# First attention of a two-layer network: norms, projections and tiles written as one hand order, output projected by tiles of 128 tokens

## The chip, the cores and the metric

The kernel runs on one core of a Trainium2 chip. The metric is the device time of one execution in microseconds (us); a single run's time and a median of several runs are both used below and always named. The core's engines run side by side, each with an instruction queue of its own that is worked off in order: TensorE (PE, matrix products; its weight loads are listed apart as PEld), VectorE (DVE), ScalarE (ACT), GpSimd (POOL), and SyncE (SP), which here only issues DMAs. PE writes to PSUM, which has eight banks of 128 partitions by 512 float32.

## What is computed

`x` has 2 sequences of 1024 tokens with 128 features, all float32. Eight residual stages follow one another: `x = x + stage(layernorm(x))`. The change touches the first only, a local attention with 16 heads of 8 features and windows of 64 tokens:

```python
def _L0_attn_a_ref(x, Wq, bq, Wk, bk, Wv, bv, Wo, bo):
    W, H = 64, 16; dh = D // H; C = L // W; scale = 1 / sqrt(dh)
    q, k, v = x @ Wq.T + bq, x @ Wk.T + bk, x @ Wv.T + bv
    # each window of 64 queries sees its own 64 keys and the 64 before them
    idx = arange(C)[:, None] * W + arange(2 * W)[None, :]
    kc, vc = (padded by W in front)[:, idx]
    scores = einsum('bcqhd,bckhd->bchqk', qc, kc) * scale   # keys before token 0 masked
    out = einsum('bchqk,bckhd->bcqhd', softmax(scores), vc)
    return out @ Wo.T + bo
```

The other seven stages (a mixture of experts, a causal attention, the experts again, a second small attention, six transformer layers, a linear attention, six layers again) stay as they are.

## The kernel before

`network` (L1712) reads `x` into four tiles `xt` of 128 features by 512 tokens (a "block"), loads the early weights, and calls the stages in turn; `attn_a0` is the first, `ffn0` follows. Most stages already write out by hand in which order each engine's instructions go (`tc.manual_schedule`); outside such a section the framework's scheduler sets the order.

`attn_a0` has two parts. The first is under the scheduler and runs over the four blocks: a layer norm (PE turns the block over to PSUM, DVE takes mean and variance, ACT a square root and DVE its reciprocal at L172 and L173, DVE subtracts and scales at L181, PE turns it back, ACT copies it to `a0xn`); the projection to queries and keys (L239), brought to SBUF with their biases by ACT (L241) and DVE (L243) as `a0both`; a DMA of `a0both` to DRAM (`a0rows`, L245) and eight DMAs back (`a0qk`, L248) that put every head's 8 features at the start of a 32 partition group; the values (L255), brought to SBUF with their bias by DVE (L259).

The second part is `Chunks`, by hand. It runs over 16 tiles of 128 tokens, 8 to a sequence, as a pipeline of calls:

- `scores`: 64 small matmuls (L874) into four banks (PSUM tag `sc`, four buffers, so one tile's scores at a time; the projections use the same tag).
- `softmax`, in two halves: per bank a maximum (L886) and a subtraction (L887) on DVE, with a mask added first (L884) in the first tile of a sequence; then an exponential of half a tile on ACT (L889).
- `sums`: DVE sums the tile (L894) and takes reciprocals (L895), POOL multiplies the two halves (L897).
- `transposes`: four times four PE transposes into a bank of tag `tp` (two buffers) and a copy by ACT to `a0pT` (L201, L907).
- `outputs`: 64 small matmuls into a bank of their own (two in turn, L918), and a copy by ACT to `a0oT` (L924).
- `project`, every fourth tile only: eight 512 column matmuls (L931) into a `tp` bank, and one DVE instruction (L933) that adds bias and result to a block's `xt`.

The probabilities `a0pr` have three buffers: tile m's can be written once tile m-3's have been transposed. In iteration n of the loop the calls are softmax(n), project(n-3), transposes(n-2), sums(n-1), scores(n+1), outputs(n-2).

Of the kernel before, what the change touches and what calls it, by code (L numbers as in the profile page):

```python
# [10 lines left out]
F32 = mybir.dt.float32  # L11
BF16 = mybir.dt.bfloat16
AF = mybir.ActivationFunctionType
ALU = mybir.AluOpType
# [3 lines left out]
P = 128  # L18
# [66 lines left out]
class Net:  # L85
# [118 lines left out]

    def attn_a0(self, key):
        nc, tc = self.nc, self.tc
        scale = 1.0 / math.sqrt(DH)  # L210
        with ExitStack() as ctx:
            wp = ctx.enter_context(tc.tile_pool(name="a0w", bufs=1))
            sb = ctx.enter_context(tc.tile_pool(name="a0s", bufs=2))
            ps = ctx.enter_context(tc.tile_pool(name="a0ps", bufs=2, space=PSUM))
            wp2 = ctx.enter_context(tc.tile_pool(name="a0av", bufs=1, space=PSUM))
            dr = ctx.enter_context(tc.tile_pool(name="a0d", bufs=4, space=bass.MemoryType.DRAM))
            w, bv, mask = self.w["a0"], self.w["a0_bv"], self.w["a0_mask"]
            wqk = w[:, 0:256].rearrange("p (s e) -> p s e", s=2)
            wv = w[:, 256:384]
            wo = w[:, 384:896].rearrange("p (g e) -> p g e", g=4)  # L220
            bqk, bo = w[:, 896:898], w[:, 898:899]

            def blk(b, k):
                return slice(WIN + 512 * k, WIN + 512 * (k + 1))

            xn, qk, v = [], [], []
            for b in range(B):
                xn.append(wp.tile([P, WIN + N], F32, tag=f"xn{b}", name=f"a0xn{b}"))
                qk.append(wp.tile([P, 4, 2, WIN + N], F32, tag=f"qk{b}", name=f"a0qk{b}"))
                v.append(wp.tile([P, N // WIN, D], F32, tag=f"v{b}", name=f"a0v{b}"))  # L230
                nc.gpsimd.memset(xn[b][:, 0:WIN], 0.0)
                nc.gpsimd.memset(qk[b][:, :, 1, 0:WIN], 0.0)
            for b in range(B):
                for k in range(2):
                    self.norm(self.xt[2 * b + k], xn[b][:, blk(b, k)], ps, f"{key}_{b}_{k}")
                    both = sb.tile([P, 2, 512], F32, tag="both", name=f"a0both{b}{k}")
                    for s in range(2):
# [26 lines left out]
            for av in avs:  # L264
                nc.vector.memset(av, 0.0)
# [558 lines left out]
    def ffn1(self, key):  # L824
        with ExitStack() as ctx:
            Layers(ctx, self, key).run()


class Chunks:


# [1044 lines left out]
```

## Time and profile before

| what | us |
|---|---|
| median of 3 runs | 4017.5 (4013.72 to 4019.96) |
| the profiled execution: time | 4017.42 |
| the profiled execution: span | 4015.3 |
| first statistics on DVE (L162) start | 12.73 |
| first score of tile 0 on PE (L874) starts | 42.70 |
| first mask of tile 0 on DVE (L884) starts | 45.36 |
| last reciprocal of tile 15 (L895) starts, takes | 189.62, 0.25 |
| last addition to `xt` (L933) starts, takes | 203.15, 0.75 |
| first transpose of the next stage (L1002) starts | 203.96 |

A page of the profile lists busy time by engine, the chain of work that ended last (each step goes back to what released it), and groups of instructions by line. A line of the timeline has the start, the busy time, engine, line, operation, `out<-in`, and in brackets how long the engine sat idle before it and what ended that. A line of the stretches has start and end, length, then busy time and number of instructions of PE, PEld, DVE, ACT and POOL, the clock granted to TensorE (1.00 is full), the share of time that the 16 DMA engines were busy, and GB/s.

### The profile page before, as it was taken

What the parts mean: (1) busy time and instruction counts of PE and PEld (TensorE: products, weight loads), DVE (VectorE), ACT (ScalarE), POOL (GpSimd) and SP (SyncE); (2) the same over time, 40 slices, a digit from 0 to 9 for tenths busy, and PEclk for the clock granted to TensorE, in tenths of its full rate; (3) what the DMA queues carried; (4) which work ended last, traced back from release to release, by engine and by line L of the source; (5) the groups of instructions that cost most, each with busy time, mean ns of one, the idle gap of its engine ahead of it and who ended that gap; (6) DMA issues with size and microseconds to landing.
All of it is one profiled execution on the core that took longest, in us unless ns stands there. A gap on an engine that the chain in (4) does not pass through costs nothing.

```text
span 4015.3 us, 156131 instructions
## 1 busy us (share of the span) xinstructions
PE 3837.7 (96%) x67292; PEld 2518.4 (63%) x67292; DVE 3132.5 (78%) x6004; ACT 2418.4 (60%) x4588; POOL 2492.4 (62%) x1614
## 2 busy tenths in 40 slices
PE   6798979999999999999999879999999999999998
PEld 4545435666666666666666436666666666666665
DVE  6876777888887888878787577787878787878786
ACT  3534437766666666666666447666666666666665
POOL 1432338776766676767765267766766767667662
PEclk8899989999999999999999779999999999999999
DMA  3020322232232332322222022332322323322222
GB/s 87 2 68 17 73 73 60 70 87 74 71 91 69 76 86 74 85 70 74 69 70 68 12 86 69 76 85 75 86 71 74 92 67 77 83 75 69 65 68 55
DMA packets 217398, 281.11 MB, mean 70 GB/s; under 512 B 52494, under 2 KB 108683, under 8 KB 216587
## 3 DMA queue, kind: packets, MB, share of 16 engines
q1 hardware_dynamic: 216714, 271.12, 26.7%
q8 instruction: 536, 8.78, 0.9%
q14 instruction: 148, 1.20, 0.1%
HBM read 69.46 MB, written 3.28 MB: 18 GB/s over the span
## 4 chain that ended last, share of the span: by engine, by line
PE 86%; DVE 7%; DMA 2%; ACT 2%; issue 1%; POOL 1%; SPq 0%; DVEq 0%; POOLq 0%; ACTq 0%
PE pj_l L1358 17%; PE y_l L1589 9%; PE pv_l L1460 9%; PE tqk_l L201 9%; PE av_l L1557 8%; PE sc_l L1507 7%; PE tpr_l L201 4%; PE to_l L201 4%; PE fy_l L1699 3%; PE fg_l L1663 3%; PE fa_l L1684 3%; PE sc_l L1498 2%; DMA f0share_e<-f0d_e 1%; DVE a0pr L887 1%; DVE a0mx L886 1%
## 5 line engine op out<-in xcount | busy, mean ns | idle before, releaser
L1387 DVE TENSOR_TENSOR t_l<-pj_l,rot_l 128x512 f32<-128x512 f32 x1536 | 967.7, 684 | 368.5 <-ACT sq_l L1367 356.9
L1404 POOL TENSOR_TENSOR raw_l<-t_l,t_l 128x1024 f32<-128x1024 f32 x384 | 908.4, 2366 | 527.2 <-DVE on_l L1565 356.3
L1358 PE MATMUL pj_l<-wqkv_l,x_l 128*128 128x512 f32 x1536 | 784.9, 614 | 6.7 <-DVE t_l L1387 4.0
L1419 POOL TENSOR_TENSOR raw_l<-raw_l,rn_l 128x1024 f32<-128x1024 f32 x384 | 723.1, 1901 | 94.5 <-ACT rn_l L1414 87.0
L1393 POOL TENSOR_TENSOR sq_l<-sq_l 128x512 f32<-128x512 f32 x384 | 490.8, 1278 | 310.7 <-ACT sq_l L1367 307.5
L1367 ACT ACTIVATE sq_l<-pj_l 128x512 f32<-128x512 f32 x768 | 461.5, 603 | 367.8 <-PE pj_l L1358 360.5
L201 PE MATMUL tqk_l<-ident_sb,raw_l 128*128 128x128 f32 x3072 | 452.5, 278 | 15.3 <-POOL raw_l L1419 13.6
L1437 ACT COPY qT_l<-tqk_l 128x512 f32<-128x512 f32 x384 | 224.8, 585 | 387.0 <-PE tqk_l L201 386.8
L201 PEld LDWEIGHTS tqk_l<-ident_sb,raw_l 128*128 128x128 f32 x3072 | 356.1, 142 | 160.2 <-issue 122.1
L1460 PE MATMUL pv_l<-wqkv_l,x_l 128*128 128x512 f32 x768 | 415.8, 623 | 5.9 <-DVE ln_xn_fl L1643 5.4
L1589 PE MATMUL y_l<-outT_l,wo_l 128*128 128x128 f32 x3072 | 393.7, 281 | 0.0
L1507 PEld LDWEIGHTS sc_l<-kT_l,qT_l 64*32 64x32 f32 x24576 | 295.4, 105 | 155.2 <-issue 144.8
L1589 PEld LDWEIGHTS y_l<-outT_l,wo_l 128*128 128x128 f32 x3072 | 357.5, 191 | 18.2 <-issue 1.0
L1358 PEld LDWEIGHTS pj_l<-wqkv_l,x_l 128*128 128x128 f32 x1536 | 256.1, 192 | 172.0 <-issue 111.6
L1557 PE MATMUL av_l<-vw_l,pT_l 64*32 64x64 f32 x24576 | 359.9, 224 | 2.1 <-issue 1.9
L1469 ACT COPY v_l<-pv_l 128x512 f32<-128x512 f32 x384 | 225.1, 586 | 224.6 <-PE pv_l L1460 204.1
L1565 DVE TENSOR_TENSOR on_l<-av_l,inv_l 128x512 f32<-128x512 f32 x384 | 247.5, 686 | 119.5 <-PE av_l L1557 119.2
L1557 PEld LDWEIGHTS av_l<-vw_l,pT_l 64*32 64x32 f32 x24576 | 294.2, 105 | 70.0 <-issue 63.2
L1507 PE MATMUL sc_l<-kT_l,qT_l 64*32 64x64 f32 x24576 | 329.7, 223 | 0.0
L201 PEld LDWEIGHTS tpr_l<-ident_sb,pr_l 128*128 128x128 f32 x1536 | 189.1, 141 | 152.1 <-issue 116.4
L1517 DVE TENSOR_TENSOR pr_l<-sc_l,mx_l 128x512 f32<-128x512 f32 x384 | 265.5, 692 | 13.2
L1516 DVE TENSOR_REDUCE mx_l<-sc_l 128x8 f32<-128x512 f32 x384 | 261.4, 681 | 3.3 <-PE sc_l L1507 3.3
(319 smaller groups left out, 6111.9 us busy)
## 6 DMA issues: line engine op xcount, KB each, us to landing
vw_l<-v_l SPq DMA_DIRECT2D x3024, 64.0 KB
wqkv_l<-in_Wqkv SPq DMA_DIRECT2D x36, 512.0 KB
f0share_e<-f0d_e SPq DMA_DIRECT2D x64, 256.0 KB
rot_l<-in_rotary SPq DMA_DIRECT2D x24, 512.0 KB
wo_l<-in_Wo SPq DMA_DIRECT2D x12, 512.0 KB
w_l<-in_W SPq DMA_DIRECT2D x12, 341.0 KB
a0rows<-a0both SPq DMA_DIRECT2D x4, 512.0 KB
a0qk<-a0rows SPq DMA_DIRECT2D x32, 64.0 KB
```

The costliest lines, as they stand in the source:

```text
L201: self.nc.tensor.transpose(tp[:, c, :], src(c), self.ident)
L1358: self.nc.tensor.matmul(pj.rearrange("p h d -> p (h d)"), self.x[b][0][:, ts(a, P)], self.w[i]["qkv"][:, ds(INNER * s + 512 * u, 512)], st ...
L1367: self.nc.scalar.activation(st["sq", s][:, u], st["pj", s, u], AF.Square)
L1387: self.nc.vector.tensor_tensor(to, st["pj", s, u], tabs[:, k, None, ts(w, LD // 2)].to_broadcast(half), ALU.mult)
L1393: self.nc.gpsimd.tensor_tensor(sq[:, 0], sq[:, 0], sq[:, 1], ALU.add)
L1404: self.nc.gpsimd.tensor_tensor(r.rearrange("p h u d -> p u h d"), st["t1", s], st["t2", s], ALU.add)
L1419: self.nc.gpsimd.tensor_tensor(r, r, st["rn"][:, ts(s, LH), None].to_broadcast([P, LH, LD]), ALU.mult)
L1460: self.nc.tensor.matmul(pj, self.x[b][0][:, ts(a, P)], self.w[i]["qkv"][:, ds(2 * INNER + 512 * r, 512)], start=True, stop=True,)
L1507: nc.tensor.matmul(sc[j][ts(c, 32), hp, :], st["q"][rows, hp, ts(c, 32)], st["k"][rows, hp, ds(32 * c, 64)], start=False, stop=(hp == 7),)
L1517: nc.vector.tensor_tensor(p, st["sc"][j], mx[:, :, None].to_broadcast([P, 8, 64]), ALU.subtract)
L1557: nc.tensor.matmul(av[r][ts(c, 32), q, j, :], st["pT", j][rows, q, ts(c, 32)], st["vw"][rows, c, ts(2 * q + j, LD)], start=True, stop=True,)
L1589: self.nc.tensor.matmul(y[:, 0:P], self.w[i]["o"][:, c, :], st["o"][:, c, :], start=(c == 0), stop=(c == 7))
```

## The change

`Chunks` takes over the first part too. Every piece of work of one engine becomes a method with a short name, and a string `A0_ORDER` lists them all; inside the hand-ordered section each engine works off its own words in that order. Words end in the block (0 to 3) or tile (0 to 15), and where there are several pieces in a letter: `sf`, `tp`, `cp` have four (a to d), `ex`, `ml`, `pv`, `ev` two.

- PE: `Tin`, `Tx` (the norm's transposes), `pk`, `pq` (keys and queries), `pv` (values), `S` (scores), `tp`, `av` (outputs), `y` (output projection).
- DVE: `sta`, `dev` (norm), `ek`, `ev` (keys and values out of PSUM), `sf` (mask, maximum, subtraction of one bank), `sm` (sum, reciprocal), `ya` (addition to `xt`).
- ACT: `fx` (norm to SBUF), `eq`, `ex` (exponential), `cp` (copy to `a0pT`), `oc` (copy of the outputs). POOL: `rs` (inverse root), `ml` (product). SP: `dw` (to DRAM), `dl` (eight DMAs back).

What differs beside the order: the norm's inverse root is taken by POOL with a power instead of by ACT and DVE; the maxima of each bank get a small tile of their own; the outputs are copied to a tile of 128 tokens (two buffers) and projected tile by tile, 16 times eight 128 column matmuls, each with a DVE addition of 128 columns; the bank for it is one of the two `tp` banks as before. The two output banks are set to zero at the start. Numbers of buffers are otherwise the same.

```diff
     def attn_a0(self, key):
-        nc, tc = self.nc, self.tc
-        scale = 1.0 / math.sqrt(DH)
         with ExitStack() as ctx:
-            wp = ctx.enter_context(tc.tile_pool(name="a0w", bufs=1))
...
-            avs = [wp2.tile([P, 4, P], F32, tag=f"av{i}", name=f"a0av{i}") for i in range(2)]
-            for av in avs:
-                nc.vector.memset(av, 0.0)
-            with tc.manual_schedule(engines=ORDERED):
-                Chunks(self, [x[:, :, 0, WIN:] for x in qk], [x[:, :, 1, :] for x in qk], v, wo, bo, avs, mask, scale, sb, ps).run()
+            chunks = Chunks(ctx, self)
+            with self.tc.manual_schedule(engines=ORDERED):
+                chunks.run()
...
+A0_ORDER = """
+    Tin0 Tin1 sta0 rs0 dev0 Tx0 fx0 pk0 sta1 ek0 pq0 rs1 dev1 pv0b Tin2 Tx1 eq0 dw0 fx1 pv0a pk1
+    ev0b sta2 pq1 rs2 ev0a pv1a ek1 dl0 dev2 ev1a pv1b eq1 Tin3 Tx2 ev1b sta3 S0 sf0d sf0c ex0b
+    sf0b fx2 sf0a S1 dw1 rs3 dev3 sf1a ex0a Tx3 sf1d fx3 sf1b pq3 sf1c eq3 S2 sm0 ml0b ex1a ex1b
+    sf2a sf2b pk2 tp0d ml0a ek2 pq2 sf2c cp0d dl1 tp0b cp0b eq2 pv2b tp0a tp0c cp0a ex2a sf2d ev2b
+    sm1 S3 sf3b cp0c ex2b sf3a sf3c ml1a sf3d tp1b av0 sm2 cp1b ml1b tp1d ex3a ml2a cp1d ex3b tp1c
+    S4 cp1c sf4c tp1a tp2b sf4a cp1a sf4b cp2b pv3a ev3a ml2b tp2a tp2d sf4d oc0 sm3 cp2a dw2 tp2c
+    S5 sf5a sf5b ml3b sf5c ex4b av1 ml3a pv2a cp2d tp3a cp2c ex4a cp3a sf5d dl2 y0 ev2a tp3b S6 sm4
+    ex5b cp3b ml4b oc1 av2 ya0 sf6d sf6b ex5a tp3c tp3d cp3c cp3d tp4c tp4d cp4c cp4d y1 sf6c sf6a
+    ml4a tp4b ex6a S7 oc2 sm5 ya1 av3 ml5b sf7d tp4a cp4b cp4a y2 sf7c tp5c sf7a pk3 av4 ex6b sf7b
+    ml5a ex7a ek3 ya2 S8 sm6 cp5c ex7b ml6b tp5b tp5a cp5b oc3 dw3 cp5a sf8c tp5d cp5d ml6a sf8b
+    tp6b oc4 cp6b y3 sf8d sf8a tp6c cp6c ex8a ya3 av5 S9 tp6d tp6a sm7 ml7a cp6a cp6d ex8b tp7a
+    sf9b sf9c ml7b cp7a y4 sf9d tp7c ya4 cp7c dl3 sf9a ex9b tp7d sm8 oc5 S10 av6 tp7b ex9a cp7d
+    ml8a tp8a ml8b cp7b oc6 tp8b sf10c av7 cp8a sf10b sf10d tp8d cp8b sf10a sm9 S11 cp8d tp8c sf11d
+    sf11b y5 sf11c ml9b cp8c ex10b ml9a av8 ya5 ex10a tp9c tp9b sf11a cp9c cp9b sm10 tp9d S12 ml10b
+    cp9d ml10a oc7 tp9a cp9a y6 av9 sf12d ex11a oc8 ya6 ex11b tp10c tp10d cp10c sf12a sf12b cp10d
+    tp10a sf12c sm11 tp10b ml11b cp10b S13 cp10a y7 sf13d y8 ex12b ya7 sf13b ex12a ml11a ya8 av10
+    tp11c tp11d cp11c sf13a tp11a cp11d tp11b oc9 oc10 cp11a sf13c S14 y9 sm12 sf14a ya9 sf14c
+    cp11b ml12a av11 ex13a ex13b oc11 tp12a tp12b cp12a ml12b cp12b tp12d cp12d sf14d y10 sf14b
+    tp12c sm13 S15 cp12c ml13b av12 ml13a sf15a ex14a ya10 pv3b tp13c tp13d ex14b oc12 cp13c sm14
+    cp13d tp13a ml14a tp13b sf15b ml14b sf15d sf15c cp13a y11 cp13b tp14b ex15a av13 ya11 tp14a
+    ex15b ev3b cp14b cp14a tp14d sm15 cp14d ml15a tp14c y12 cp14c ml15b av14 tp15b ya12 oc13 tp15a
+    cp15b cp15a tp15c cp15c tp15d cp15d oc14 y13 ya13 av15 oc15 y14 y15 ya14 ya15
+"""
...
 class Chunks:
...
+    def __init__(self, ctx, net):
+        self.net, self.nc, self.st = net, net.nc, {}
+        nc, tc = net.nc, net.tc
+        self.pool = ctx.enter_context(tc.tile_pool(name="a0c", bufs=1))
+        self.sb = ctx.enter_context(tc.tile_pool(name="a0s", bufs=2))
+        self.ps = ctx.enter_context(tc.tile_pool(name="a0ps", bufs=1, space=PSUM))
+        self.dr = ctx.enter_context(tc.tile_pool(name="a0d", bufs=4, space=bass.MemoryType.DRAM))
+        w = net.w["a0"]
+        self.wqk = w[:, 0:256].rearrange("p (s e) -> p s e", s=2)
+        self.wv = w[:, 256:384]
+        self.wo = w[:, 384:896].rearrange("p (g e) -> p g e", g=4)
+        self.bqk, self.bo = w[:, 896:898], w[:, 898:899]
+        self.scale = 1.0 / math.sqrt(DH)
+        self.xn, self.qk, self.v = [], [], []
+        for b in range(B):
+            self.xn.append(self.pool.tile([P, WIN + N], F32, tag=f"xn{b}", name=f"a0xn{b}"))
+            self.qk.append(self.pool.tile([P, 4, 2, WIN + N], F32, tag=f"qk{b}", name=f"a0qk{b}"))
+            self.v.append(self.pool.tile([P, N // WIN, D], F32, tag=f"v{b}", name=f"a0v{b}"))
+            nc.gpsimd.memset(self.xn[b][:, 0:WIN], 0.0)
+            nc.gpsimd.memset(self.qk[b][:, :, 1, 0:WIN], 0.0)
+        self.avs = [self.ps.tile([P, 4, P], F32, tag=f"av{i}", name=f"a0av{i}") for i in range(2)]
+        for av in self.avs:
+            nc.vector.memset(av, 0.0)
     def run(self):
...
+        for word in A0_ORDER.split():
+            name, m, z = re.fullmatch("([A-Za-z]+?)([0-9]+)([a-d]?)", word).groups()
+            getattr(self, name)(int(m), *(["abcd".index(z)] if z else []))
+    def bank(self, name, tag="tp", shape=(P, 4, P)):
+        bufs = {"sc": 4, "tp": 2}[tag]
+        self.st[name] = self.ps.tile(list(shape), F32, tag=tag, name=f"a0{name}", bufs=bufs)
+        return self.st[name]
+    def tl(self, tag, m, bufs=2, shape=(P, 4, P)):
+        self.st[tag, m] = self.sb.tile(list(shape), F32, tag=tag, name=f"a0{tag}{m}", bufs=bufs)
+        return self.st[tag, m]
+    def cols(self, k):
+        return slice(WIN + 512 * (k % 2), WIN + 512 * (k % 2 + 1))
...
+    def sta(self, k):
+        nc, small = self.nc, self.net.small
+        s = small.tile([P, 4, 6], F32, tag="ln_st", name=f"a0st{k}")
+        mv = self.st["mv", k] = small.tile([P, 4, 2], F32, tag="ln_mv", name=f"a0mv{k}")
+        for c in range(4):
+            nc.vector.bn_stats(s[:, c, :], self.st[f"in{k}"][:, c, :])
+            nc.vector.bn_aggr(mv[:, c, :], s[:, c, :])
+    def rs(self, k):
+        rs = self.st["rs", k] = self.net.small.tile([P, 4], F32, tag="ln_rs", name=f"a0rs{k}")
+        self.nc.gpsimd.tensor_scalar_add(rs, self.st["mv", k][:, :, 1], EPS)
+        self.nc.gpsimd.tensor_tensor(rs, rs, self.net.nhalf, ALU.pow)
+    def dev(self, k):
+        x, mv = self.tl("dev", k), self.st["mv", k]
+        for c in range(4):
+            self.nc.vector.tensor_scalar(
+                x[:, c, :], self.st[f"in{k}"][:, c, :], mv[:, c, 0:1], self.st["rs", k][:, c : c + 1],
+                ALU.subtract, ALU.mult,
+            )
...
+    def dw(self, k):
+        rows = self.st["rows", k] = self.dr.tile([P, 2, 512], F32, tag="rows", name=f"a0rows{k}")
+        self.nc.sync.dma_start(rows, self.st["both", k])
+    def dl(self, k):
+        for s in range(2):
+            for j in range(4):
+                self.nc.sync.dma_start(
+                    self.qk[k // 2][ds(32 * j, DH), :, s, self.cols(k)],
+                    self.st["rows", k][ts(j, 32), s, :].rearrange("(g d) t -> d g t", g=4),
+                )
...
+    def S(self, m):
+        qk, a = self.qk[m // NT], m % NT
+        banks = [self.bank(f"s{m}{j}", "sc") for j in range(4)]
         for g in range(4):
             for c in range(2):
                 t0 = P * a + WIN * c
                 for j in range(4):
                     rows = slice(32 * j, 32 * j + DH)
                     self.nc.tensor.matmul(
...
+                        banks[j][ts(c, WIN), g, :], qk[rows, g, 0, ds(WIN + t0, WIN)],
+                        qk[rows, g, 1, ds(t0, 2 * WIN)], start=True, stop=True,
                     )
...
+    def sf(self, m, j):
+        nc, src = self.nc, self.st[f"s{m}{j}"]
+        if ("p", m) not in self.st:
+            self.tl("p", m, 3, (P, 16, P))
+        s = self.st["p", m][:, ts(j, 4), :]
+        mx = self.net.small.tile([P, 4], F32, tag="mx4", name=f"a0mx{m}{j}")
+        if m % NT == 0:
+            mask = self.net.w["a0_mask"]
+            nc.vector.tensor_tensor(s, src, mask[:, None, :].to_broadcast([P, 4, P]), ALU.add)
+            src = s
+        nc.vector.tensor_reduce(mx, src, AX.X, ALU.max)
+        nc.vector.tensor_tensor(s, src, mx[:, :, None].to_broadcast([P, 4, P]), ALU.subtract)
+    def ex(self, m, h):
+        p = self.st["p", m][:, ts(h, 8), :]
+        self.nc.scalar.activation(p, p, AF.Exp, scale=self.scale)
+    def sm(self, m):
+        sm = self.st["sm", m] = self.net.small.tile([P, 16], F32, tag="sm16", name=f"a0sm{m}")
+        self.nc.vector.tensor_reduce(sm, self.st["p", m], AX.X, ALU.add)
+        self.nc.vector.reciprocal(sm, sm)
+    def ml(self, m, h):
+        p = self.st["p", m][:, ts(h, 8), :]
+        self.nc.gpsimd.tensor_tensor(
+            p, p, self.st["sm", m][:, ts(h, 8), None].to_broadcast([P, 8, P]), ALU.mult
+        )
+    def tp(self, m, j):
+        tp = self.bank(f"t{m}{j}")
+        for g in range(4):
+            self.nc.tensor.transpose(tp[:, g, :], self.st["p", m][:, 4 * j + g, :], self.net.ident)
+    def cp(self, m, j):
+        self.nc.scalar.copy(self.tl("pT", f"{m}{j}", 6), self.st[f"t{m}{j}"])
+    def av(self, m):
+        v, av = self.v[m // NT], self.avs[m % 2]
         for g in range(4):
             for c in range(2):
                 for j in range(4):
...
+                    self.nc.tensor.matmul(
+                        av[ds(32 * j, DH), g, ts(c, WIN)], v[:, 2 * (m % NT) + c, ts(4 * g + j, DH)],
+                        self.st["pT", f"{m}{j}"][:, g, ts(c, WIN)], start=True, stop=True,
                     )
...
+    def oc(self, m):
+        self.nc.scalar.copy(self.tl("o", m), self.avs[m % 2])
+    def y(self, m):
+        y = self.bank(f"y{m}", shape=(P, P))
+        for g in range(4):
+            self.nc.tensor.matmul(
+                y, self.wo[:, g, :], self.st["o", m][:, g, :], start=(g == 0), stop=(g == 3)
+            )
+    def ya(self, m):
+        x = self.net.xt[m // 4][:, ts(m % 4, P)]
+        self.nc.vector.scalar_tensor_tensor(x, self.st[f"y{m}"], self.bo, x, ALU.add, ALU.add)
```

## The prediction

> **What bounds the kernel now.** The page first, then the stretch that the change touches.
>
> ```profile
> span 4015.3 us, 156131 instructions
> PE 3837.7 (96%) x67292; PEld 2518.4 (63%) x67292; DVE 3132.5 (78%) x6004; ACT 2418.4 (60%) x4588; POOL 2492.4 (62%) x1614
> ```
>
> TensorE's 96% is a mean over the whole program; the first attention is only the first 204 us of 4015, so the whole answer lies within some 5%. I cut those 204 us into stretches: norms and projections, softmax of the 16 tiles, tail.
>
> ```profile
> 12.70:45.40 32.70, 25.33 (x172) 16.57 (x172) 18.95 (x65) 8.62 (x14) 0.00 (x0) 0.95 0.63 176
> 45.40:189.90 144.50, 101.79 (x2106) 75.13 (x2107) 130.85 (x171) 69.56 (x102) 54.78 (x30) 0.79 0.07 12
> 189.90:204.00 14.10, 11.51 (x169) 7.33 (x167) 0.75 (x1) 5.62 (x10) 5.17 (x3) 0.96 0.01 2
> ```
>
> Third busy column: in the middle stretch VectorE works 130.85 of 144.50 us, with short starts between instructions almost all of it. It sets the pace there, and it is idle for 14 us of the first stretch and nearly all of the last. A plain tile takes VectorE 7.8 us (sums begin at 59.57, 67.29, 75.08): four banks of 1.32 (maximum plus subtraction, 55.60 to 56.93) and 2.48 for sum and reciprocal (59.57 to 62.05). Its waits inside the stretch, from its timeline:
>
> ```profile
> 95.92 0.69 DVE L887 TENSOR_TENSOR a0pr<-a0sc,a0mx 128x512 f32<-128x512 f32 x1
> 99.05 0.75 DVE L933 SCALAR_TENSOR_TENSOR xt<-a0y,a_sb,xt 128x512 f32<-128x512 f32 x1 [2.44 <-PE a0y L931]
> ```
>
> Three times 2.44 for the output projection (at 96.6, 136.2, 171.3) and four for scores (0.63, 0.58, 0.65, 0.58): 9.7 us. The tail, from the chain of waits:
>
> ```profile
> 187.61 3.76 POOL a0pr L897 x2
> ...
> 199.41 3.71 PE a0y L931 x8
> 203.13 0.03 issue
> 203.15 0.76 DVE xt L933
> ```
>
> **Head: softmax starts earlier.** Tile 0 needs block 0's queries and keys alone, yet its scores start at 42.70, behind all four blocks' products. In the new order they wait for SP's DMAs of block 0, and I price that by its queue.
>
> ```profile
> 22.26 0.33 SPq L245 DMA_DIRECT2D a0rows<-a0both  x1
> 24.90 2.72 SPq L248 DMA_DIRECT2D a0qk<-a0rows  x8
> ...
> 54.65 2.68 SPq L248 DMA_DIRECT2D a0qk<-a0rows  x8
> ```
>
> The write of block 0 (22.26) lands at 24.90; a step moved in time keeps its nine DMAs. The eight reads of block 3, alone on the queues, go out from 54.65 and the DMA engines fall quiet near 63: 8.3 us for 512 KB. For block 0: 24.9 + 8.3 = 33.2. From below 32.2 (72 GB/s from 36 to 48 us makes 7.3), from above 35.5, when block 1's first read went out behind a write that queued behind block 0's reads. Scores at half clock take 2.0 (83.95), so the first mask starts at 33.2 + 2.1 = 35.3 instead of 45.36: **-10.1**.
>
> VectorE's work ahead of it fits in: from 12.73, four `sta` of 1.65 (two in 3.3 from 204.71, with this alternating order; 1.37 now), three `dev` of 1.38, two `ek` of 0.75, four `ev` of 0.69, together 15.0, with 2.7 of waits for `rs0` and `pk0` ends near 30.4. The 4.9 us left until 35.3 hide the slower statistics; without this cover they would cost 1.1. The inverse root on POOL takes 1.35 (206.51 to 207.86), against 1.9 for table load, root and reciprocal in block 0 (14.10 to 16.02), so the write still goes out near 22.3. POOL is idle there. What `S0` holds up on PE (`S1`, `Tx3`, `pq3`) and `sf0` on VectorE (`dev3`) is later work of blocks 2 and 3; block 1's reads are needed only by tile 4, near 68 us, behind 25 us of cover, and blocks 2 and 3 by tile 8, past 100.
>
> What VectorE has not done by then follows between tiles: one `dev` 1.4, two `ek` 1.5, four `ev` 2.8: **+5.7**.
>
> **Middle.** The three projection waits and four score waits go with their order: **-9.7**. VectorE's additions: 16 of 128 columns instead of 4 of 512. The nearest rows of that size are 0.285 (L415, bank plus SBUF) and 0.351 (L408); I take 0.29, the same shape of inputs. Twelve fall before tile 15's sums: 3.5 against three of 0.67: **+1.5**.
>
> The new waits are the uncertain term. The first `sf` of tile m needs a probability buffer, so all transposes of tile m-3. In the old loop those preceded `S(m)`. In the new one PE's words run `S6 av2 tp3c tp3d`, `S7 av3 tp4a`, `S8 tp5b tp5a tp5d`, `S10 av6 tp7b`, and so on: transposes behind scores that cannot start before VectorE leaves the last `sc` bank. At full clock `S` is 1.21 (75.28), `av` 1.1, four transposes 0.53 (eight in 1.07); at half 2.01, 1.9, 0.97. Tile 6: 1.35 + 1.1 + 1.07 + 0.15 = 3.7 against the 2.8 of `sm4 ya0` that cover it: wait 0.9; at half clock 6.2, wait 3.4. Likewise tiles 7 to 12: 0.4, 0.35, 0, 0.7, 0, 0 at full and 2.4, 2.4, 1.5, 2.7, 0.8, 0.8 at half clock; sums 2.3 and 14.0. Before tile 5, projections run between tiles while PE has little to do; the clock was 0.50 from 48 to 68 us, and I count 3.3 there (`S1` 0.9, `pk2` 0.8, `tp1a` 1.6). The bounds are 2.3 and 17.3; below nothing is excluded, since the sum so far has VectorE without a wait. Which clock?
>
> ```profile
> 78.62:82.03 3.41, 1.49 (x20) 1.07 (x20) 3.34 (x6) 2.21 (x4) 2.92 (x2) 0.95 0.00 0
> 82.03:85.45 3.42, 3.38 (x64) 3.07 (x72) 3.33 (x4) 2.40 (x4) 0.00 (x0) 0.50 0.02 5
> 85.45:88.86 3.41, 3.41 (x95) 2.87 (x80) 2.71 (x5) 0.59 (x1) 3.26 (x2) 0.55 0.02 5
> ```
>
> A stretch of 3.4 us with PE busy for 44% of it is followed by two at half clock; at 0.79 on average, 42% of the middle ran so. The new tiles give PE 5.3 us at full clock (1.2 + 1.1 + 2.1 + 0.9) where three of four had 4.4, so such thin stretches become rarer, not gone. I take a fifth: 2.3 + 0.2 x 11.7 + 3.3 = **+8.0**.
>
> The Trainium skill ("TensorE: Matmul & The Clock Gate", "Why this matters for your kernels") asks only that PE not pause for more than about 3 us between bursts. Here PE's longest pause before the drop at 82 us was 1.3 us (80.83 to 82.08), so the row contradicts it. By the rule the tiles would stay at full clock, and the sum would be 4006 instead of 4008.
>
> **Projection by 128 columns.** Eight instructions of 512 took 3.70 (95.31); eight of 128 take 0.89 in the causal attention (365.96, clock 1.00), four times 0.89 is 3.6, so PE's sum is unchanged, with 96 more instructions.
>
> The same page ("Back-to-back issue gap") speaks against narrow products: about 81 ns each in a stream at 128 columns, 131 ns at 512, so four narrow ones cost 2.5 times one wide one. By that a `y` would be 2.2 us, the two at the end 2.6 us more, the sum 4011; the rows of 0.89 say otherwise.
>
> **Tail.** Before, 14.0 us from tile 15's last reciprocal (189.87) to 203.91: POOL still had tile 14 to multiply, and a 3.71 projection of four tiles ended it. The new order takes `sm14` three banks ahead of `sm15`, so POOL starts tile 15 at once: 4.0, transposes and copy until `y13` finds a bank 1.3, `y13` 0.9, `av15` 1.1, `y14` 0.9, `y15` 0.9, additions and starts 0.4: 9.5, **-4.5**. The next stage's first transpose stood 0.05 behind the last addition; it could now follow `y15` directly (0.8 earlier at best); I count nothing.
>
> **Sum.** -10.1 + 5.7 - 9.7 + 1.5 + 8.0 - 4.5 = -9.1. The profiled execution took 4017.42 (2.1 more than its span), the median of the runs 4017.5: the same. Forecast **4008**, its own range 4004 to 4012.5. Within 0.2%, 8 us, is about what a measurement of this kernel can't tell from no change: the border lies at 4009.5.
>
> **Rivals.**
> PE stays at full clock: waits 3.3 instead of 8.0, scores of tile 0 in 1.2: 4003. For it: denser PE work in each tile. Against it: 42% at half clock now. Chance 0.20.
>
> The new wait takes the place of the old: half clock in most tiles, waits near 15, and block 0's reads landing at 35.5: 7 + 2.3 given back, 4017.5. For it: each late transpose also thins PE's next stretch. Chance 0.19.
>
> Slower: PE becomes the bound. At half clock a tile costs PE 2.0 + 1.9 + 3.9 + 1.7 = 9.5 against VectorE's 8.1; sixteen are 152, the projections of blocks 2 and 3 another 13 (twice their 6.6), and some 1 us a tile until scores may start, over 12 tiles 12. From 35.3 that ends at 213, 9.5 behind now: 4027. It decides from about two thirds of the stage at half clock (5.3 + 4.2 s = 8.1), a granted clock under 0.67, where 0.79 is measured. Chance 0.08.
>
> **How the numbers follow.** Forecast 0.53, of which 0.37 lies below 4009.5; rivals 0.20, 0.19, 0.08. Faster 0.37 + 0.20 = 0.57; within 0.2% 0.16 + 0.18 = 0.34; slower 0.09. Range 3999 to 4019: it takes in the waits' ends and leaves out the slow rival.
>
> **What would show it.** The first mask near 35.3; no wait of 2.44 at `ya`; VectorE waits before `sf6` to `sf12` on transposes, 5 to 11 us in all; last reciprocal near 185; next stage's first transpose near 195. Wrong would be a first mask past 40 (reads late), a mean clock under 0.7 from 35 to 185 us, or VectorE waiting on ScalarE or POOL in mid-stage.

## The result, and the profile after

| | before | after |
|---|---|---|
| median of 22 runs each, us | 4018.16 (4009.71 to 4037.5) | 4006.18 (3997.29 to 4020.8) |
| ratio of after to before, 95% interval | | 0.9971 (0.9963 to 0.9979) |
| profiled execution: time; span | 4017.42; 4015.3 | 4006.44; 4004.7 |
| first mask of tile 0 on VectorE starts | 45.36 | 38.16 |
| last reciprocal of tile 15 ends | 189.87 | 180.88 |
| next stage's first transpose starts | 203.96 | 190.84 |

The changed kernel is faster by 12 us (8.4 to 14.9 by the interval). The stretches of the first attention, cut as before at the first statistics, the first mask, the last reciprocal and the next stage; columns as in the stretches before the prediction:

```profile
12.70:38.16 25.46, 16.45 (x127) 10.87 (x125) 13.60 (x50) 2.55 (x4) 5.06 (x8) 0.89 0.58 182
38.20:180.90 142.70, 103.24 (x2241) 81.28 (x2242) 135.10 (x190) 73.38 (x110) 56.78 (x30) 0.86 0.10 20
180.90:190.80 9.90, 7.85 (x173) 6.66 (x171) 1.40 (x4) 3.50 (x7) 3.75 (x2) 1.00 0.01 2
```

The head is 7.2 us shorter and the tail 4.1. The middle is only 1.8 shorter: VectorE (third busy column) has 4 us more to do in it, since work of blocks 2 and 3 now stands there, but less to wait for. The chain of waits of the changed kernel tells what sets the first mask (start, length, what):

```profile
18.86 3.76 PE a0p L888 x4
...
23.36 2.61 DMA a0rows<-a0both
...
28.06 7.19 DMA a0qk<-a0rows
...
36.10 2.04 PE a0s L948 x58
```

Block 0's way to DRAM and back is the whole of it, as forecast: products, write, reads, scores. VectorE's timeline says so from the other side, in the bracket of the first mask:

```profile
38.16 0.69 DVE L962 TENSOR_TENSOR a0p<-a0s,a_mask_sb 128x512 f32<-128x512 f32 x1 [6.67 <-PE a0s L948]
...
91.01 0.69 DVE L965 TENSOR_TENSOR a0p<-a0s,a0mx 128x512 f32<-128x512 f32 x1 [0.21 <-PE a0t L987]
```

It had nothing to do for 6.67 us. The second line is the new wait that the forecast was unsure of, in tile 6: a subtraction that needs a probability buffer and so waits for the transposes of tile 3. Here it is 0.21. All waits of VectorE of 0.15 or more between first mask and last reciprocal come to 3.9 us, where 8.0 were forecast.

### The profile page after: what moved, and what is told of

It reads as the page before. It is cut to its first block, busy times and chain, and to the rows that moved or that the text cites. A ratio compares the mean times of both kernels' runs of the same rounds, so it can differ in the third digit from the quotient of the medians.

```text
span 4004.7 us, 156308 instructions
## 1 busy us (share of the span) xinstructions
PE 3821.0 (95%) x67388; PEld 2516.4 (63%) x67388; DVE 3133.1 (78%) x6012; ACT 2414.2 (60%) x4582; POOL 2498.2 (62%) x1622
## 4 chain that ended last, share of the span: by engine, by line
PE 86%; DVE 7%; DMA 2%; POOL 1%; issue 1%; ACT 1%; SPq 0%; DVEq 0%; POOLq 0%; ACTq 0%
PE pj_l L1439 17%; PE y_l L1670 9%; PE pv_l L1541 9%; PE tqk_l L202 9%; PE av_l L1638 8%; PE sc_l L1588 7%; PE tpr_l L202 4%; PE to_l L202 4%; PE fy_l L1780 3%; PE fg_l L1744 3%; PE fa_l L1765 3%; PE sc_l L1579 2%; DMA f0share_e<-f0d_e 1%; DVE a0p L965 1%; DVE a0mx L964 1%
## 5 line engine op out<-in xcount | busy, mean ns | idle before, releaser
L202 PE MATMUL tqk_l<-ident_sb,raw_l 128*128 128x128 f32 x3072 | 452.6, 278 | 15.6 <-POOL raw_l L1500 14.1
L202 PEld LDWEIGHTS to_l<-ident_sb,on_l 128*128 128x128 f32 x1536 | 183.2, 141 | 128.5 <-issue 111.0
```

The costliest lines, as they stand in the source:

```text
L202: self.nc.tensor.transpose(tp[:, c, :], src(c), self.ident)
```

## The experiments

Each ratio is to runs of the kernel before taken beside it. "Stage end" is the start of the next stage's first transpose; "middle" runs from the first mask to the end of the last reciprocal, and its waits are VectorE's of 0.15 us or more.

| kernel | ratio to before (95%) | first mask | middle | of it waits | tail | stage end |
|---|---|---|---|---|---|---|
| before, three profiles | 1 | 45.36, 46.06, 45.31 | 144.5, 145.2, 144.5 | 9.8, 11.4, 10.8 | 14.1, 14.9, 14.1 | 203.96, 206.12, 203.94 |
| after, three profiles | 0.9971 (0.9963 to 0.9979) | 38.16, 38.52, 37.69 | 142.7, 149.0, 154.0 | 3.9, 9.9, 13.5 | 10.0, 10.0, 10.0 | 190.84, 197.47, 201.66 |
| before, addition late | 0.9988 (0.9979 to 0.9997) | 45.28 | 137.3 | 3.4 | 15.2 | 197.70 |
| after, projection by 512 | 1.0 (0.9991 to 1.0009) | 37.59 | 153.6 | 14.3 | 12.1 | 203.29 |
| after, all blocks first | 0.998 (0.9971 to 0.9988) | 42.05 | 144.5 | 9.2 | 10.0 | 196.48 |
| after, four buffers | 0.9963 (0.9951 to 0.9975) | 37.65 | 145.0 | 5.2 | 10.0 | 192.63 |
| after, block 2 first | 0.9964 (0.9951 to 0.9977) | 37.37 | 146.0 | 9.5 | 10.0 | 193.32 |
| before, projection by 128 | 1.001 (1.0002 to 1.0019) | 46.34 | 154.7 | 17.3 | 10.9 | 211.97 |
| after, filler products | 0.9963 (0.9949 to 0.9976) | 38.77 | 146.6 | 7.5 | 10.0 | 195.34 |
| after, tile 14's sums late | not timed | 38.09 | 149.7 | 10.7 | 13.6 | 201.42 |

The two unchanged kernels were profiled three times each; the other rows are single profiles and are to be read against that scatter. A stage end of the changed kernel between 190 and 202 tells nothing by itself, while its tail and its first mask hardly move. Nor is a profiled execution always a typical one: that of the late addition was the fastest of its eleven runs, that of the projection by 512 the slowest of its ten.

### The addition alone, late, in the kernel before

```diff
             do(self.softmax, n, 0)
             do(self.project, n - 3)
             do(self.transposes, n - 2, 0)
             do(self.softmax, n, 1)
+            do(self.add, n - 3)
```

> The kernel before, with the DVE addition of the output projection issued half an iteration later (after the second half of the next tile's maxima) and nothing else changed. Theory (the three waits of 2.44 us for the projection are VectorE standing in line for it too early, and cost what they show): the next stage's first transpose moves from 203.96 by -7.3 to 196.6, and the three waits are gone; whole time about -7 us, ratio 0.998. Rival (the projection of 512 columns blocks PE for 3.7 us and the wait comes back before the next maxima, because transposes and scores are late): no more than -2, with VectorE waits for scores or transposes in their place.

VectorE's timeline of this kernel around the first of the three places:

```profile
99.09 0.74 DVE L937 SCALAR_TENSOR_TENSOR xt<-a0y,a_sb,xt 128x512 f32<-128x512 f32 x1
99.74 2.28 DVE L895 TENSOR_REDUCE a0sm<-a0pr 128x16 f32<-128x2048 f32 x1
102.05 0.25 DVE L896 RECIPROCAL a0sm<-a0sm 128x16 f32<-128x16 f32 x1
103.05 0.69 DVE L887 TENSOR_REDUCE a0mx<-a0sc 128x4 f32<-128x512 f32 x1 [0.74 <-PE a0sc L875]
```

The addition has no bracket: it waits for nothing any more. In its place the next score wait is 0.74, three times. The middle is 7.3 to 7.9 us shorter than before's; the tail is 1.1 longer, so the stage ends 6.3 earlier than the first profile of before, where 7.3 were expected. The theory held. The time is 0.9988, so some 5 us (1.2 to 8.4 by the interval) were to be had by moving one line, without the new head.

### The new order with the old projection

```diff
     def oc(self, m):
-        self.nc.scalar.copy(self.tl("o", m), self.avs[m % 2])
+        if m % 4 == 0:
+            self.tl("o", m // 4, 2, (P, 4, 512))
+        self.nc.scalar.copy(self.st["o", m // 4][:, :, ts(m % 4, P)], self.avs[m % 2])
     def y(self, m):
-        y = self.bank(f"y{m}", shape=(P, P))
+        if m % 4 != 3:
+            return
+        y = self.bank(f"y{m}", shape=(P, 512))
...
     def ya(self, m):
-        x = self.net.xt[m // 4][:, ts(m % 4, P)]
+        if m % 4 != 3:
+            return
+        x = self.net.xt[m // 4]
```

> The changed kernel with the output projection put back to 512 columns once per four tiles, at the place of the fourth tile's words. Theory (128 columns pay mainly in the tail; in the middle the place of the addition in the order is what removed the waits): the next stage's first transpose moves from 190.84 by about +2.5 (tail 9.96 to about 12.2, VectorE has 9 fewer additions before the last sum, -1.5, and waits for the 3.7 us projection come to +1 to 2). Rival (projecting tile by tile is what removed the 2.44 waits): +7 or more, three waits of over 2 us before the additions.

VectorE's additions in this kernel:

```profile
161.52 0.75 DVE L1020 SCALAR_TENSOR_TENSOR xt<-a0y,a_sb,xt 128x512 f32<-128x512 f32 x1 [1.98 <-PE a0y L1012]
...
187.34 0.75 DVE L1020 SCALAR_TENSOR_TENSOR xt<-a0y,a_sb,xt 128x512 f32<-128x512 f32 x1 [2.78 <-PE a0y L1012]
...
202.49 0.75 DVE L1020 SCALAR_TENSOR_TENSOR xt<-a0y,a_sb,xt 128x512 f32<-128x512 f32 x1 [11.32 <-PE a0y L1012]
```

With the new order kept and only the width undone, the gain is gone: 1.0, and the intervals of this and of the changed kernel stand well apart. Two waits before additions came back (1.98 and 2.78, where the changed kernel has 0.71 to 0.97), and the tail is 12.1 instead of 10.0. These are some 5 us of the 11.7 that the ratios show; the rest of the difference lies in a middle that has the waits of the changed kernel's slowest profile, and one profile can't say whether the width or chance put them there. The waits are more than the theory's 1 to 2 us and fewer than the rival's three of over 2 us; in the whole time the rival came true.

### More of the norms ahead of tile 0: all blocks, or block 2 alone

All blocks first: the words of blocks 2 and 3 stand ahead of `S0`, and `a0both` gets four buffers. Block 2 first: only its own words move.

```diff
-    ... sta3 S0 sf0d sf0c ex0b sf0b fx2 sf0a S1 dw1 rs3 dev3 ... (blocks 2 and 3 between tiles 0 to 15)
+    ... sta3 fx2 rs3 pk2 pq2 dev3 ek2 eq2 pv2a Tx3 ev2a pv2b fx3 ev2b pk3 pq3 ek3 eq3 pv3a ev3a pv3b ev3b S0 ...
```

```diff
+    ... sta3 fx2 rs3 pk2 pq2 ek2 eq2 dev3 pv2a ev2a S0 ...
```

> The changed kernel with the norm, projection and values of blocks 2 and 3 moved ahead of tile 0's scores in the order, as the kernel before had them, and four buffers instead of two for the projected block (so that the key and query copies don't wait for a DMA). Theory (tile 0 waits for its DMAs, not for PE or VectorE, so VectorE's 6.67 us of idle time before the first mask is free, and the early start of tile 0 in the changed order earns nothing by itself): first mask at 38 to 39.5, next stage's first transpose from 190.84 by -4 to -6. Rival (the gain of the change came from starting tiles ahead of blocks 2 and 3; the later blocks' DMAs delay block 0's reads): first mask past 41, next stage +1 to +3.

> The changed kernel with the norm, products, key and value copies of block 2 (fx2 rs3 pk2 pq2 ek2 eq2 dev3 pv2a ev2a) ahead of tile 0's scores, and nothing else moved; block 3 stays where it is. VectorE idles 6.67 us in front of the first mask (38.16 us, it was done at 31.49) because block 0's reads land only at 35.25. Theory: this idle time holds 2.8 us of VectorE work (two ek of 0.70, one dev of 1.38 less its share already there, one or two ev of 0.69) that now stands between tiles; moving all four blocks forward was too much (first mask 42.05), moving one fits: first mask 38.2 to 38.7, next stage's first transpose at 187 to 189 instead of 190.84, ratio about 0.9965. Rival: the extra TensorE products (pk2 pq2 pv2a, 3.2 us at full clock, up to 6 at half) and the copies' waits reach past the reads, as they did with four blocks: first mask 39.5 to 41, next stage's first transpose at 191 to 193, ratio 0.9975 to 0.998.

VectorE with all blocks first, up to the first mask:

```profile
33.88 1.36 DVE L872 TENSOR_SCALAR a0dev<-a0in,a0mv,a0rs 128x128 f32<-128x128 f32 x4 [1.47 <-POOL a0rs L867]
...
39.22 0.69 DVE L933 TENSOR_TENSOR a0v<-a0v,a_bv_sb 128x512 f32<-128x512 f32 x1 [1.00 <-PE a0v L928]
...
42.05 0.69 DVE L962 TENSOR_TENSOR a0p<-a0s,a_mask_sb 128x512 f32<-128x512 f32 x1 [1.25 <-PE a0s L948]
```

And with block 2 alone:

```profile
35.44 0.68 DVE L933 TENSOR_TENSOR a0v<-a0v,a_bv_sb 128x512 f32<-128x512 f32 x1
37.37 0.69 DVE L962 TENSOR_TENSOR a0p<-a0s,a_mask_sb 128x512 f32<-128x512 f32 x1 [1.25 <-PE a0s L948]
```

The idle 6.67 us do not hold all of it: VectorE waits for roots and products in between (the brackets 1.47 and 1.00), and the first mask came 3.9 us later. The expectation fell. The rival had the lateness right and its cause wrong: the chain of waits runs over TensorE's products and transposes from 20 us to the first scores at 40.86, with short steps of ScalarE and VectorE between, and over no DMA. The idle time does hold block 2: the first mask is at 37.37, no later than the 37.69 to 38.52 of the changed kernel, with 1.25 of idle time left in front of it. What that frees in the middle is smaller than the scatter: the ratio came as expected (0.9964), the stage end did not (193.32, not 187 to 189). The intervals of both ratios (0.998 and 0.9964) overlap the changed kernel's, so these runs don't show either that the early start of tile 0 is worth time by itself.

### A fourth buffer for the probabilities

```diff
-            self.tl("p", m, 3, (P, 16, P))
+            self.tl("p", m, 4, (P, 16, P))
```

> The changed kernel with four buffers of probabilities instead of three. Theory (VectorE's waits of 0.21, 0.21, 0.56 and 0.34 us before tiles 6, 7, 8 and 10 are the buffer's): these four go, next stage's first transpose -1.0 to -1.5. Rival (they turn into waits for scores or banks a moment later): 0, the same sum of waits under another name.

At tile 6 VectorE now has this:

```profile
91.11 0.69 DVE L964 TENSOR_REDUCE a0mx<-a0s 128x4 f32<-128x512 f32 x1 [1.11 <-PE a0s L948]
91.90 0.69 DVE L965 TENSOR_TENSOR a0p<-a0s,a0mx 128x512 f32<-128x512 f32 x1
```

All waits for transposes (`a0t`) are gone from its timeline, so they were the buffer's, as the prediction had it. Part of them came back as waits for scores (1.11, 0.65) and for projections (1.00 twice); 5.2 us in all. The 1.0 to 1.5 us that were expected at the stage's end can't be seen, since 192.63 lies within the scatter, and the ratio of 0.9963 can't be told from the changed kernel's 0.9971.

### The new projection in the old order

Here the projection of a tile stands between the two halves of the next tile's transposes, and its addition between the softmax and the sums; the first part is untouched.

```diff
             do(self.softmax, n, 0)
-            do(self.project, n - 3)
             do(self.transposes, n - 2, 0)
+            do(self.project, n - 3)
             do(self.softmax, n, 1)
+            do(self.add, n - 3)
```

> The kernel before with its first part untouched (scheduler's norms, ACT and VectorE root, all four blocks ahead of tile 0), and of the change only the projection: every tile's outputs projected by eight 128 column products straight behind its outputs, with an addition of 128 columns at the end of the loop's round. Theory (the per-tile projection by itself is worth most of the middle and the tail, the new head is worth the rest): first mask at 45.4 as before, no wait of 2.44, tail 10 to 12 us instead of 14.1, next stage's first transpose at 193 to 196 instead of 203.96 (three waits 7.3 and a 3 us shorter tail, less 1.5 for sixteen small additions), ratio 0.9975 to 0.998. Rival (the late addition is what counts, the width is not): the same as the run with the late addition alone, 197.7, since score waits stay and sixteen additions cost what the tail saves; ratio 0.9985 to 0.999.

VectorE at the end of its middle:

```profile
192.38 0.25 DVE L896 RECIPROCAL a0sm<-a0sm 128x16 f32<-128x16 f32 x1
198.25 0.35 DVE L934 SCALAR_TENSOR_TENSOR xt<-a0y,a_sb,xt 128x128 f32<-128x128 f32 x1 [5.62 <-PE a0y L930]
198.52 2.28 DVE L895 TENSOR_REDUCE a0sm<-a0pr 128x16 f32<-128x2048 f32 x1
```

Both expectations fell: slower than before, 1.001. Only the tail came as the theory had it, 10.9 instead of 14.1. The addition of every tile now stands ahead of the sums on VectorE, and waits 1.14 in every other tile. Ahead of tile 15's sums it waits 5.62 for a projection that is behind transposes on TensorE, which wait for GpSimd; so GpSimd gets tile 15 8.5 us after tile 14 (192.38 to 200.83). A narrow projection is thus no gain in itself: it needs a place for its addition where the product is long done, and that is what the new order gives (`y1 S7 sm5 ya1`, for instance: a tile's scores and another's sums stand between product and addition).

### Two unchanged kernels, profiled again

> The changed kernel once more, unchanged, profiled again. It measures how far the end of the first attention differs between two profiled executions of one program. If the clock's 3.4 us windows fall by chance, the waits in the middle (3.9 us in the first profile, 8.0 forecast) and the middle's mean clock (0.86) differ: next stage's first transpose anywhere from 189.5 to 193.5, with more wait where the clock is lower. If the phase is fixed by the program, 190.84 within 0.3 us and the same waits at the same places.

> As the run before: the changed kernel, profiled a third time. By chance of the clock's windows: 189.5 to 193.5 for the next stage's first transpose, first mask 37.0 to 38.7 (block 0's products at half or full clock in the first 27 us). By a fixed phase: 190.84 and 38.16 within 0.3 us.

> The kernel before once more, unchanged, profiled again, to see how far the end of its first attention differs between two executions. If its old order (transposes ahead of the next scores) makes VectorE's waits depend little on the clock: next stage's first transpose at 202 to 206, three waits of 1.8 to 3.5 for the projection, score waits of 0.5 to 0.8, whatever the clock's windows. If it depends on them as the changed kernel does: anywhere from 198 to 211.

> As the run before, a third profile of the kernel before: 202 to 206 if the old order depends little on the clock's windows, 198 to 211 if as much as the new one.

VectorE at tile 6 in the second profile of the changed kernel, which reads 0.21 in the first:

```profile
94.16 0.69 DVE L964 TENSOR_REDUCE a0mx<-a0s 128x4 f32<-128x512 f32 x1 [1.13 <-PE a0s L948]
97.83 0.69 DVE L965 TENSOR_TENSOR a0p<-a0s,a0mx 128x512 f32<-128x512 f32 x1 [2.98 <-PE a0t L987]
```

Four stretches of 3.41 us around tile 6, first in the first profile of the changed kernel:

```profile
82.46:85.87 3.41, 1.38 (x10) 1.22 (x11) 3.34 (x6) 1.03 (x2) 3.11 (x2) 1.00 0.00 0
85.87:89.28 3.41, 3.41 (x124) 3.07 (x126) 3.38 (x4) 2.82 (x5) 0.00 (x0) 1.00 0.02 5
89.28:92.69 3.41, 2.17 (x49) 1.69 (x38) 3.13 (x7) 1.82 (x3) 2.49 (x2) 1.00 0.00 0
92.69:96.10 3.41, 2.90 (x49) 2.25 (x53) 3.34 (x6) 1.41 (x3) 1.26 (x1) 1.00 0.02 5
```

and in the second:

```profile
82.46:85.87 3.41, 1.74 (x117) 1.39 (x97) 3.27 (x5) 2.27 (x4) 1.24 (x1) 1.00 0.02 5
85.87:89.28 3.41, 1.97 (x12) 1.81 (x13) 3.31 (x6) 0.43 (x1) 2.51 (x2) 0.71 0.00 0
89.28:92.69 3.41, 3.41 (x38) 3.08 (x44) 3.38 (x4) 2.09 (x4) 0.00 (x0) 0.50 0.00 0
92.69:96.10 3.41, 3.41 (x122) 2.87 (x107) 1.02 (x3) 1.49 (x3) 3.08 (x2) 0.50 0.02 5
```

The program is the same and so are the lines; in the last two stretches the granted clock (third figure from the end) is 1.00 in one and 0.50 in the other, TensorE is then busy all of 6.8 us, and VectorE (third busy column) falls from 3.34 to 1.02 of 3.41. The mean clock from 45.4 to 181 us was 0.88, 0.82 and 0.76 in the three profiles, with waits of 3.9, 9.9 and 13.5 us. So it differs from execution to execution, by up to 11 us at the stage's end. That is more than either reading of the expectation allowed: 197.47 and 201.66 lie past 193.5. The chip doesn't explain it: the second and third profile come from the same one, and the run with tile 14's sums late, on another, has the second's waits. The kernel before varies by 2.2 us there. That is nearer to the first reading of its expectation, but 206.12 lies past 206, and one projection wait of 4.99 and one of 4.13 lie past its 3.5. That the smaller spread comes from the old order, transposes ahead of the next scores, is argued and not shown.

### Filler products on TensorE

```diff
+    def fi(self, n):
+        av = self.avs[n % 2]
+        for i in range(n // 2):
+            g, j = divmod(i % 16, 4)
+            self.nc.tensor.matmul(
+                av[ds(32 * j, DH), g, :], self.v[0][:, 0, ts(j, DH)], self.net.ident, start=True, stop=True
+            )
```

> The changed kernel with 72 extra products (8 by 128 columns, written to an output bank that is not in use, and written over by the next tile's outputs) on TensorE, ahead of pieces at which it idled 0.9 to 4 us waiting for GpSimd or VectorE: 12 ahead of tp1b and tp7a, 10 ahead of tp2b, 16 ahead of tp6b, 6 ahead of pv3a, tp3a and tp8a, 4 ahead of tp4c. The result is the reference's. Theory (the waits of tile 6 and after come from 3.4 us windows at half clock that follow a thin window): windows that were thin become 65% busy or more, the clock from 70 to 140 us stays at 0.93 or more (0.93 in the first profile of the changed kernel, about 0.8 in its second and third), the wait for transposes at tile 6 (2.98 and 2.88 in those, 0.21 in the first) stays under 1, waits in the middle 3 to 5 us, next stage's first transpose at 188 to 192, ratio 0.995 to 0.997. Rival: the clock's windows do not depend on how busy TensorE is in the window before, or the extra products themselves stand in the way (1.3 us each time at full clock, 2.7 at half): waits 10 to 18 us, next stage's first transpose at 197 to 205, ratio 0.9975 to 1.

VectorE at tile 6, and at tile 10:

```profile
92.67 0.69 DVE L965 TENSOR_TENSOR a0p<-a0s,a0mx 128x512 f32<-128x512 f32 x1 [0.21 <-PE a0t L987]
...
132.75 0.69 DVE L965 TENSOR_TENSOR a0p<-a0s,a0mx 128x512 f32<-128x512 f32 x1 [2.18 <-PE a0t L987]
```

The clock was 1.00 without a break from 72 to 113 us, and tile 6 waited 0.21, as the theory has it, and as in the first profile of the changed kernel, which had no filler. From 123 to 133 us it was at half, and tile 10 waited 2.18; from 70 to 140 us the mean clock was 0.89, where the theory asked for 0.93. Waits of 7.5 us lie between the two expectations, and the ratio of 0.9963 can't be told from 0.9971. Whether filler helps stays open.

### Tile 14's sums late

```diff
-    ... cp13c sm14 cp13d tp13a ml14a tp13b sf15b ml14b sf15d sf15c ... tp14b ... sm15 cp14d ml15a ...
+    ... cp13c cp13d tp13a tp13b sf15b sf15d sf15c ... ev3b sm14 sm15 ml14a ml14b tp14b ... ml15a ml15b ...
```

> The changed kernel with tile 14's sums right ahead of tile 15's, as in the old loop, and what hangs from them (ml14, tp14, cp14) behind. Theory (the tail is shorter because GpSimd has done tile 14 before tile 15's reciprocal): GpSimd multiplies tile 14 in 3.8 us first, so the tail from tile 15's last reciprocal to the next stage's first transpose grows from 9.96 to 13.5 to 14, with two products of GpSimd's more in it. Rival (the tail is short because the last projections are 128 columns wide, and GpSimd's lead is hidden behind tile 13's and 14's outputs): 10 to 11.

GpSimd's timeline behind tile 14's reciprocal, in this kernel:

```profile
185.54 7.46 POOL L978 TENSOR_TENSOR a0p<-a0p,a0sm 128x1024 f32<-128x1024 f32 x4 [6.23 <-DVE a0sm L974]
```

and behind tile 15's in the changed kernel:

```profile
181.05 3.75 POOL L978 TENSOR_TENSOR a0p<-a0p,a0sm 128x1024 f32<-128x1024 f32 x2 [3.86 <-DVE a0sm L974]
```

Four products in a row instead of two, and a tail of 13.6 instead of 10.0. The theory held. Up to the sums its profile has the waits of the changed kernel's second one to a few hundredths, so the 3.7 us are the order's.

## Why the prediction was right

Against the means of three profiles of each kernel:

| step | forecast | measured |
|---|---|---|
| first mask earlier | -10.1 | -7.5 (45.6 to 38.1) |
| VectorE's work in the middle (+5.7 moved, +1.5 additions) | +7.2 | +5.6 (130.2 to 135.8 busy) |
| old waits gone | -9.7 | -10.7 |
| new waits | +8.0 | +9.1 (3.9 to 13.5) |
| tail | -4.5 | -4.4 (14.4 to 10.0) |
| stage end | -9.1 | -8.0 (204.7 to 196.7) |

The measured terms sum to -7.9; the starts between instructions and the rounding are the rest. Terms and sum agree so well partly by luck: the head fell short by 2.6 us and the new waits by 1.1, the work in the middle and the old waits made up for 2.6 of it, and the mean of the new waits is one of three values as far apart as 3.9 and 13.5.

**The head's size was off by 2.6 us, its mechanism was right.** The prediction put the first mask at 35.3 from a write at 22.3, reads of 8.3 us and scores of 2.1. In the first profile the write went out at 23.36, 1.1 later, because the first products took 3.76 (2.76 before): the steps from one to the next were 1.01, 0.86, 0.85 and 0.85 us, and before 1.01, 0.72, 0.43 and 0.43. The forecast took the write over from the row before and left the clock of these products out. The reads, first issued at 25.99, landed at 35.25, 9.3 instead of 8.3. Scores and mask start took 2.9. Together 2.9 us: the case "landing at 35.5" of the second rival was the nearer end (35.25). That VectorE's own work fits in ahead held: it was done at 31.49 and idle for 6.67.

**The moved work** was 5.57 by its rows (one `dev` 1.36, two `ek` 1.49, four `ev` 2.72), as counted. The twelve additions inside the middle last 0.26 to 0.35 each, but start under the end of the instruction ahead, so that the two together made VectorE 5.6 busier and not 7.2.

**The new waits** came where they were put (before `sf6`, `sf7`, `sf8`, `sf10`, before products of blocks 2 and 3), and at tile 6 within 0.7 of the forecast for each clock: 0.9 and 3.4 forecast for full and half, 0.21 and 4.1 (1.13 for scores + 2.98 for transposes) measured. The sum had no waits before the additions; there are one or two of 0.71 to 0.97 in each profile, 1.4 in all in the mean. What the prediction treated as one value between two clocks is a spread over executions. The waits of the first two rivals, 3.3 with the clock full, and near 15 so that they eat the gain, are not other outcomes of the change but are nearly reached by single executions of it: the first profile waited 3.9 and took 4006.44, the third waited 13.5 and took 4017.01. The slower rival, TensorE as the bound, did not come: it decides from a granted clock under 0.67, and 0.76 was the lowest mean. (Its terms add up to 212.3, not 213.)

**The tail** came out in its size, and both of its causes are shown: without `sm14` ahead of `sm15` it is 3.7 us longer (13.6 against 10.0), with a wide last projection 2.1 (12.1). Together that is more than the 4.4 us gained, so the two overlap and their shares can't be told apart.

**The projection by 128 columns** was counted as free on TensorE: eight took 1.16 and sixteen 2.05 at the end of the stage, 0.13 to 0.15 each, starts included. (The forecast's 0.89 is eight steps of 0.11 and leaves out the end of the last product; with it the same eight take 1.06 from 365.80, while its 3.70 for wide ones has the end in it. Step by step, 0.11 against 0.43, four narrow ones cost what one wide one does.) By an estimate from the figures of the Trainium skill ("TensorE: Matmul & The Clock Gate", "Back-to-back issue gap") narrow ones would have cost 2.6 us in the tail; the steps of 0.11 and 0.43 here speak against these figures. Undoing the narrow ones cost 11.7 us. What the prediction did not say is that the new order depends on them.

**What stays open.** The means at the stage's end differ by 8.0 us, the medians of 22 runs by 12.0 (8.4 to 14.9). What follows the stage took 3811.3, 3811.6 and 3809.1 us before and 3813.9, 3808.0 and 3813.5 after, so these profiles don't show the missing 4 us there. But that part scatters too: in all fourteen profiles it runs from 3805.0 to 3814.7, and the second profile of the changed kernel, whose stage ended 6.6 us later than the first's, took only 0.8 longer as a whole. Of the 22 runs only three took over 4015, and one of the three profiles did; three profiles are too few for a mean of something that spreads over 11 us. How the 12 us divide among the early start, the place of the additions, the narrow projection and the tail stays open as well: undoing the width alone takes all of them, so the parts don't add up.

## What to carry to other kernels

Price a moved start by its whole chain, with each transfer from issue to landing and each product at the clock that it will really get, and take the late end of each. On an in-order engine, an instruction that waits for another engine goes where its input is long done: one late addition was worth some 5 us here, and sixteen small ones in the wrong place turned the narrow projection into a loss of some 4. Before explaining a few us between two profiles, profile each kernel again: here one program's stage end spread over 11 us and the other's over 2.

## What the runs showed of the hardware that was not expected

**The clock** changes only on a grid of 3.41 us that keeps its phase through an execution (transitions of the first profile at 32.7, 60.0, 66.8, 70.2, 111.2, 114.6 and so on). The same grid does not give the same clock: in the first two profiles of the changed kernel it lies within 0.03 us at the same place, the second's first products start 0.6 us later (19.49 against 18.86), and from 60.0 us on the clocks part. The third has another phase. Stretches of the second profile cut on its grid (those around tile 6 above lie across it):

```profile
73.66:77.07 3.41, 1.62 (x68) 1.21 (x57) 3.21 (x6) 1.55 (x3) 1.91 (x2) 1.00 0.09 13
77.07:80.48 3.41, 3.37 (x16) 3.37 (x17) 2.44 (x4) 1.07 (x2) 1.84 (x1) 0.50 0.00 0
100.96:104.37 3.41, 2.36 (x115) 1.84 (x117) 3.38 (x4) 1.53 (x2) 0.00 (x0) 1.00 0.01 2
104.37:107.79 3.42, 3.12 (x38) 2.83 (x25) 2.69 (x7) 1.97 (x3) 2.65 (x2) 0.50 0.02 5
```

A drop to half clock (third figure from the end) follows a stretch with TensorE busy for 1.62 us, and one with 2.36. In all fourteen profiles, from 20 to 200 us, every full-clock stretch with TensorE busy for 1.65 us or less (48% of it) was followed by half clock, none over 2.87 was, and in between both happened. That is no rule for the whole program: in the third profile of the kernel before, a stretch with 1.42 us was followed by full clock, and one that was busy throughout by half clock:

```profile
2365.18:2368.60 3.42, 1.42 (x4) 0.35 (x2) 0.81 (x2) 3.21 (x4) 3.11 (x2) 1.00 0.00 0
2368.60:2372.01 3.41, 0.66 (x4) 0.42 (x4) 2.65 (x5) 2.56 (x6) 3.03 (x2) 1.00 0.00 0
549.29:552.70 3.41, 3.41 (x16) 1.61 (x15) 1.75 (x5) 3.06 (x6) 0.82 (x1) 1.00 0.00 0
552.70:556.12 3.42, 3.42 (x6) 1.67 (x6) 3.18 (x13) 0.47 (x2) 0.00 (x0) 0.50 0.00 0
```

So something besides TensorE's busy time in one stretch decides; what, was not found.

**The record of the granted clock begins late.** Its first entry is at 22.44 us in the first profile of the changed kernel and at 20.24 in that of the kernel before, and the views count time without an entry as 1.00. The products tell otherwise: up to the first entry those of 512 columns follow one another by 0.85 us or more, behind it by 0.43. So the 0.89 of the head above is too high, and this is most of the 1.1 us by which block 0's write was late.

**A subtraction of VectorE's can wait for a product of GpSimd's.** In the masked tiles, 0 and 8, the subtraction reads and writes SBUF only. In tile 0 GpSimd is idle, and all 56 in fourteen profiles took 0.69 us. In tile 8 a product of GpSimd's often runs beside it, as here in the kernel before (two products, the second until 116.63):

```profile
112.88 3.75 POOL L897 TENSOR_TENSOR a0pr<-a0pr,a0sm 128x1024 f32<-128x1024 f32 x2 [4.04 <-DVE a0sm L895]
114.81 2.37 DVE L887 TENSOR_TENSOR a0pr<-a0pr,a0mx 128x512 f32<-128x512 f32 x1
```

Eighteen subtractions of tile 8 took longer than 0.69, 0.94 to 2.37, and every one of them ended 0.54 to 0.55 us behind the end of such a product. The same subtraction reading scores from PSUM takes 0.69 beside GpSimd's products too. It costs VectorE 0.3 to 1.7 us an execution, in both kernels.
